# Image 1's front stepped inside image 0's depthwise convolution, in a two-layer metaformer kernel

## The chip, the cores and the metric

The kernel runs on one core of a Trainium2 chip. The metric is device time in microseconds (us) from launch to end; the shown time of a kernel is the median of its runs. A core has five engines with a queue each, and each works through its queue in order: PE (TensorE, matrix multiplies and transposes), DVE (VectorE), ACT (ScalarE), POOL (GpSimd, which here also issues the indirect DMAs) and SP (SyncE, which issues most other DMAs).

## The reference, cut to what matters

Input is x, 4 images of 384 channels by 32 x 32 points (1024 tokens an image). Two layers follow each other:

```python
# layer 0
x = x + attention(ln_c(x))            # 8 heads, relative tables, projection w_proj + b_proj
t = to_tokens(x)
t = t + gelu(ln_t(t) @ kron(c_fc_1, c_fc_2).T) @ kron(c_proj_1, c_proj_2).T
x = from_tokens(t)
# layer 1
y = ln_c(x)
x = x + dw7x7(y) + dw5x3(y) + dw3x5(y) + dw1x7_7x1(y) + dw1x5_5x1(y) + bias
t = to_tokens(x)
p = softmax(ln_t(t) @ gate_w + gate_b)            # 4 experts, the top two kept, renormalised
t = t + sum over the two experts of p * (gelu(ln_t(t) @ w1[e]) @ w2[e])
```

All five depthwise convolutions together are one 7 x 7 depthwise convolution per channel: 49 taps.

## The kernel before, in words

The first 1500 us or so are attention. All that the change touches is in `rest_phase`, which does the rest for one image after another. Channels lie on partitions in three chunks of 128 (`KC`); an image's tile `xb` is 128 x 3 x 1024, its two halves of 512 tokens are worked one after the other.

For each image:

- **front**: `loads` brings the attention output (`at`) and the image (`xb`). `project` does nine matmuls for a half (`proj_ps`, L977) and adds the result to `xb` on DVE (L980, three times); `token_stats` transposes rows on PE (`row_ps`, L87), takes statistics on DVE (L89, L90), a square root on ACT (L96). `net` spreads the scales over partitions (`all_ps`, L117, from `s_dg`, L115), then does the small network of layer 0: `u_ps` (L999, L1001), twelve f matmuls (L1012) with a gelu each on ACT (L1022), twelve o matmuls (L1016), three ffn matmuls (L1029) and adds on DVE (L1030).
- **normalise**: statistics again and `xc` (L1061), the centred half. **image** writes `xc` times its scale into `img` (L1068), the padded image. There is one `img` for all images, so an image's write stands behind the last tap of the image before.
- **convolve**: DVE adds the bias (L1080), then runs 49 taps in place, a multiply-add per chunk and tap (L1085). For images 0 to 2 a store to `x2_d` follows (L1094).
- **gates**: gate matmuls (L661), logits (L673), statistics of the rows, softmax and the choice of two experts on DVE. **scatter**: the slot of each token (`pos`, L778), the list of blocks (`block_list`), and sixteen indirect DMAs on POOL (L1197) that write the normalised rows into their slots.
- **blocks**: a block is 128 slots of one expert. An indirect DMA fetches rows (L1241), PE transposes them (`xT_ps`, L1254), two indirect DMAs fetch weights (L1260), then twelve rounds of three matmuls into `e_ps` (L1292), a gelu on ACT (L1295) and one matmul into `y_ps` (L1270); DVE adds the bias (`yo`, L1273), SP stores it. There are 67 blocks, in groups of 13, 16, 16 and 22. A group holds the blocks that the images up to its own fill; what isn't full goes to the next. So group 1 needs image 1's scatter.

Image 0 is special (`first`). DVE does chunk 0 (32 rows of 32 points) and 4 rows (`own`) of chunk 1: 36 of 96 rows. The other 60 are done by PE (`taps_by_matmul`), in four parts: two of 16 rows of chunk 2, and two of 14 rows of chunk 1. A part is 49 taps by two halves of the partitions, 98 matmuls with 64 x 64 diagonals (`tap_ps`, L1129). At its end ACT copies the two sums (L1139), PE joins them (`taps_ps`, L1140), ACT copies that (L1144) and POOL adds it to `xb` (L1145). The sums, the joins and the blocks share the PSUM pool `ps_y` ("y" twice, "t" once).

Images 1 to 3 run as `others`, a generator that is stepped from within other work. Two things set the order. Python runs the generators and so writes the program; a scheduler then orders the instructions of each engine when the kernel is built, within their dependencies. In the part with blocks, each round calls `more`, which adds 1.36 to one clock and lets `others` run until its own steps' costs (what they yield) reach it. In `others` the convolution of image b carries, from its third tap on, the dispatch (gates and scatter) of image b - 1, and from its 13th tap on the front and normalisation of image b + 1. Image 1's front and normalisation stand at the head of `others`: two steps of it (its loads) run within image 0's convolution, the rest within image 0's dispatch, three steps per step of that.

The names: `halves` is the list of (xc, scale) that `normalise` fills and `image` uses; `preload(wts[1])` fetches block weights into the tiles that held the tap diagonals; `banks` in `net` lists the PSUM banks that the f matmuls rotate through, six for images 0 and 1 and three for images 2 and 3.

Of the kernel before, what the change touches and what calls it, by code (L numbers as in the profile page):

```python
# [1 line left out]

# [1 line left out]

# [14 lines left out]
P = 128  # L19
# [874 lines left out]
def rest_phase(tc, cst, x, ao_d, ins, xs_d, y_d, x2_d, out):  # L894
# [9 lines left out]
    with ExitStack() as es:  # L904
# [82 lines left out]

        def net(b, xs, rstd):

            banks = [(ps_h, "h", None)] * 3 + ([(ps_y, "y", 2)] * 2 + [(ps_y, "t", None)] if b <= 1 else [])  # L990
            if True:
                scale = to_partitions(nc, (small, ps_m, "m"), ident, one, rstd)
                scale_sb = work.tile([P, TOK], F32, tag="scale", name="scale")
                nc.scalar.copy(scale_sb, scale)


                ps = ps_m.tile([P, TOK], F32, tag="m", name="u_ps")
                for k in range(KC):
                    nc.tensor.matmul(ps, fold[:, k, :], xs[:, k, :], start=(k == 0), stop=(k == KC - 1))  # L999
                u = small.tile([P, TOK], F32, tag="u", name="u")  # L1000
                nc.vector.tensor_tensor(u, ps, scale_sb, ALU.mult)  # L1001
                yield 1.4, 3.5

                po = ps_m.tile([P, TOK], F32, tag="m", name="o32_ps")
                pend = []
                for f0 in range(0, NF + 3, 3):
                    phs = []
                    for f in range(f0, min(f0 + 3, NF)):
                        pool, tag, bufs = banks[f % len(banks)]
                        ph = pool.tile([P, TOK], F32, tag=tag, name="f_ps", **({"bufs": bufs} if bufs else {}))  # L1010
                        lo = f % 4 * 32
                        nc.tensor.matmul(ph, c1t[lo : lo + 32, f // 4, :], u[lo : lo + 32, :], start=True, stop=True)  # L1012
                        phs.append((f, ph))
                    for f, hs in pend:
                        lo = f % 4 * 32
                        nc.tensor.matmul(  # L1016
                            po[lo : lo + 32, :], cp1t[:, f, :], hs, start=(f < 4), stop=(f >= NF - 4)
                        )
                    pend = []
                    for f, ph in phs:  # L1020
                        hs = hid.tile([P, TOK], F32, tag="hs", name="hs", bufs=HS)
                        nc.scalar.activation(hs, ph, AF.Gelu)  # L1022
                        pend.append((f, hs))
                    yield 0.0, 2.2
                o32 = small.tile([P, TOK], F32, tag="u", name="o32")
                nc.scalar.copy(o32, po)
                for m in range(KC):
                    ps = ps_h.tile([P, TOK], F32, tag="h", name="ffn_ps")
                    nc.tensor.matmul(ps, spread[:, m * P : (m + 1) * P], o32, start=True, stop=True)  # L1029
                    nc.vector.scalar_tensor_tensor(  # L1030
                        xs[:, m, :], ps, cp2[:, m : m + 1], xs[:, m, :], ALU.mult, ALU.add
                    )
                yield 2.1, 2.7
# [31 lines left out]
        def image(halves):  # L1065
            rows = IMG // 2
            for half, (xc, scale_sb) in enumerate(halves):
# [5 lines left out]
                )  # L1073
                yield 1.7, 0.0

        def convolve(b, xb, parts):


            for k in range(KC):
                nc.vector.tensor_scalar_add(xb[:, k, :], xb[:, k, :], cbias[:, k : k + 1])  # L1080
            acc = xb.rearrange("p k (y x) -> p k y x", x=IMG)
            for dy in range(7):
                for dx in range(7):
                    for k, y0, y1 in parts:
                        nc.vector.scalar_tensor_tensor(  # L1085
                            acc[:, k, y0:y1], img[:, k, dy + y0 : dy + y1, dx : dx + IMG],
                            w7[:, k, dy, dx : dx + 1], acc[:, k, y0:y1], ALU.mult, ALU.add,
                        )

                    if b:  # L1090
                        tc.keep_in_program_order(nc.vector.memset(pause, 0.0))
                    yield sum(0.12 + 0.0337 * (y1 - y0) for _, y0, y1 in parts) + 0.06, 0.0
            if b + 1 < B:
                nc.sync.dma_start(x2_d[:, b * N : (b + 1) * N].rearrange("(k p) n -> p k n", p=P), xb)  # L1094
# [10 lines left out]
        def taps_by_matmul(xb, parts):  # L1105
# [15 lines left out]
            for k, y0, ny in parts:  # L1121
                n = ny * IMG
                sums = [ps_y.tile([P, TOK], F32, tag="y", name="tap_ps", bufs=2) for _ in range(2)]
                for t0 in range(0, 49, 2):
                    for t in range(t0, min(t0 + 2, 49)):
                        dy, dx = divmod(t, 7)
                        for h in range(2):
                            lo = 64 * h
                            nc.tensor.matmul(  # L1129
                                sums[h][64 * (t % 2) : 64 * (t % 2) + 64, :n].rearrange("p (y x) -> p y x", x=IMG),  # L1130
                                diag[k][lo : lo + 64, t, :],
                                img[lo : lo + 64, k, dy + y0 : dy + y0 + ny, dx : dx + IMG],
                                start=(t < 2), stop=(t > 46),
                            )
                    yield
                po = ps_y.tile([P, TOK], F32, tag="t", name="taps_ps")
                for h in range(2):
                    e = hid.tile([P, TOK], F32, tag="hs", name="taps", bufs=HS)
                    nc.scalar.copy(e[:, :n], sums[h][:, :n])  # L1139
                    nc.tensor.matmul(po[64 * h : 64 * h + 64, :n], half, e[:, :n], start=True, stop=True)  # L1140
                yield
                acc = xb[:, k, y0 * IMG : y0 * IMG + n]
                e = hid.tile([P, TOK], F32, tag="hs", name="taps", bufs=HS)
                nc.scalar.copy(e[:, :n], po[:, :n])  # L1144
                nc.gpsimd.tensor_tensor(acc, acc, e[:, :n], ALU.add)  # L1145
                yield

        def new(shape, name, dt=F32):
# [213 lines left out]
                    yield 0.3, 0.1  # L1362
                finish(b, n0, xr, zs)

        xbs = {}

        def enter(b):
            xbs[b] = xp_.tile([P, KC, N], F32, tag="xb", name="xb")
            yield from front(b, xbs[b])

        def dispatch(b, pause=0.0):
            yield from gates(b)
            yield from scatter(b, pause)

        def first(halves):


            half, own = IMG // 2, 4
            rest = (IMG - own) // 2
            taps = taps_by_matmul(  # L1380
                xbs[0], [(2, 0, half), (2, half, half), (1, own, rest), (1, own + rest, rest)]
            )
            next(taps)
            yield from image(halves)
            for _ in convolve(0, xbs[0], [(0, 0, IMG), (1, 0, own)]):
                for _ in range(3):
                    next(taps, None)
                yield
            for _ in taps:
                pass  # L1390
            preload(wts[1])

        def others():
# [1 line left out]

            def ahead(b, halves):
                if b < B:
                    yield from enter(b)  # L1400
                    yield from normalise(xbs[b], halves)

            halves, side = [], iter(())
            yield from ahead(1, halves)
            for b in range(1, B):
                yield from image(halves)
                reached.add(b)
                halves = []
                later = ahead(b + 1, halves)
                for t, cost in enumerate(convolve(b, xbs[b], [(k, 0, IMG) for k in range(KC)])):  # L1410
                    for start, steps in ((2, side), (12, later)):
                        more = next(steps, None) if t >= start else None
# [2 lines left out]
                    yield cost  # L1415
                yield from side
                yield from later
                side = dispatch(b, 0.0 if b + 1 < B else 2.6)
            yield 6.0, 0.0
            yield from side  # L1420

        for k in range(KC):
            nc.vector.tensor_scalar_mul(fold[:, k, :], fold[:, k, :], cf2[:, k : k + 1])
        center(nc, ps_m, "m", one, fold)
        xbs[0] = xp_.tile([P, KC, N], F32, name="xb", tag="xb")
        xs0, xs1 = halves_of(xbs[0])
        halves = []
        at0, at1 = result(loads(0, xbs[0]))
        preload(wts[0], pin)
        rstd0 = result(project(xs0, at0))  # L1430
        rstd1 = result(project(xs1, at1))
        result(net(0, xs0, rstd0))
        side = normalise(xbs[0], halves, (0,))
        for _ in net(0, xs1, rstd1):
            next(side, None)
        result(side)
        result(normalise(xbs[0], halves, (1,)))
        nc.gpsimd.memset(img, 0.0)
        for _ in combined:
            pass  # L1440
        center(nc, ps_m, "m", one, gw)
        reached = set()
        todo = others()
        for i, _ in enumerate(first(halves)):
            if 6 <= i < 8:
                next(todo)
        for i, _ in enumerate(dispatch(0)):
            for _ in range(3 if i > 5 and 1 not in reached else 0):
                next(todo)
        clock = [0.0, 0.0]  # L1450

        def spend(steps):
# [126 lines left out]
```

## Time and profile before

| what | value |
|---|---|
| median of 3 runs | 3124.05 us (3121.32 to 3129.54) |
| the profiled execution | 3131.71 us |
| its span, first to last instruction | 3129.8 us |
| granted TensorE clock, mean | 0.973 |
| PE busy | 2944.8 us, 94% |
| DVE busy | 1924.3 us, 61% |
| ACT busy | 1381.9 us, 44% |
| POOL busy | 1223.7 us, 39% |

In the profiled execution image 0's convolution begins at about 1588 us and its gates at 1688.2; the first round of a block starts at 1775.7, group 1's at 2110.0. In the 344 us from 2110 to 2454 PE is busy 334.6 us.

How to read what follows. A row of a timeline or of the groups has the engine, the line of the kernel, the operation, then output <- inputs by the program's names, then partitions x elements of output and input, then how many instructions are pooled in the row. In a timeline the first two numbers are the start and the time to the end of the last of the pooled instructions, in us from the start of the span; the bracket is the idle time before and the instruction that ended it. A row of windows has a stretch and its length, and for PE, weight loads (PEld), DVE, ACT and POOL the busy time with the number of instructions; then the granted clock of PE as a share of full speed, the share of time the DMA engines were busy, and GB/s. A PE instruction in float32 appears as two records.

### The profile page before, as it was taken

The numbers are of one execution on the slowest core, as the hardware profiler recorded it, in microseconds if no ns is written. First come the engines' busy times: TensorE is split into PE (matmuls) and PEld (weight loads), VectorE is DVE, ScalarE is ACT, GpSimd is POOL, SyncE is SP. The second block draws the span as 40 slices with busy tenths as digits, with TensorE's granted clock in tenths as the row PEclk, the third lists the DMA queues.
The fourth block names the chain that finished last, engine by engine and source line by source line (L and its number), as shares of the span: only waits on it lengthen the run. The fifth ranks groups of instructions, "written<-read, shape, count | busy, mean of one in ns | idle before, by whom it ended". The sixth has DMA issues, their size and how long they took to land.

```text
span 3129.8 us, 63805 instructions
## 1 busy us (share of the span) xinstructions
PE 2944.8 (94%) x25591; PEld 2040.5 (65%) x25591; DVE 1924.3 (61%) x3572; ACT 1381.9 (44%) x2845; POOL 1223.7 (39%) x1136
## 2 busy tenths in 40 slices
PE   8997999999999999999898889989999899999996
PEld 4544777777777776777443354764777677777775
DVE  2226787878787878787485499999999500001101
ACT  1105767666666666666312313333343332333332
POOL 2224747474746464646243221230253322114412
PEclk9998999999999999999999889999999899999998
DMA  3796566666565646563412131630454145366742
GB/s 125 260 319 201 134 202 136 204 133 202 133 204 131 210 125 204 131 206 101 160 54 94 64 114 74 257 112 8 172 187 162 49 165 207 143 251 225 289 175 73
DMA packets 262792, 500.56 MB, mean 160 GB/s; under 512 B 134736, under 2 KB 186832, under 8 KB 254816
## 3 DMA queue, kind: packets, MB, share of 16 engines
q1 hardware_dynamic: 169168, 247.12, 25.5%
q0 software_dynamic: 43424, 227.84, 19.7%
q10 hardware_dynamic: 49904, 21.53, 3.5%
q8 instruction: 201, 3.29, 0.4%
q14 instruction: 95, 0.78, 0.1%
HBM read 543.58 MB, written 152.37 MB: 222 GB/s over the span
## 4 chain that ended last, share of the span: by engine, by line
PE 73%; DVE 9%; issue 8%; POOL 4%; DMA 3%; ACT 2%; another core or an unknown queue 1%; SPq 0%; POOLq 0%; DVEq 0%; ACTq 0%
PE e_ps L1292 15%; PE y_ps L1270 14%; PE t_ps L410 8%; PE sc_ps L227 7%; PE av_ps L227 7%; PE tabq_ps L227 6%; DVE xb L1085 5%; PE a_ps L420 4%; PE qk_ps L175 3%; PE tv_ps L227 2%; POOL xb L1145 2%; PE tabk_ps L227 1%; PE v_ps L186 1%; PE row_ps L87 1%; DVE oT L479 1%
## 5 line engine op out<-in xcount | busy, mean ns | idle before, releaser
L1292 PEld LDWEIGHTS e_ps<-xT,w 128*128 128x128 f32 x4824 | 658.5, 194 | 232.5 <-issue 20.4
L353 POOL TENSOR_TENSOR bias<-b,s 128x416 f32<-128x416 f32 (+24 forms) x656 | 659.4, 1044 | 172.9 <-DMA s<-sd 152.7
L1292 PE MATMUL e_ps<-xT,w 128*128 128x128 f32 x4824 | 677.0, 278 | 21.3 <-DVE xb L980 8.0
L1270 PE MATMUL y_ps<-w,eh 128*128 128x384 f32 x1608 | 655.0, 492 | 18.6 <-ACT eh L1295 16.7
L1295 ACT ACTIVATE eh<-e_ps,w 128x128 f32<-128x128 f32 x804 | 292.9, 367 | 762.8 <-PE e_ps L1292 696.4
L1085 DVE SCALAR_TENSOR_TENSOR xb<-img,pack,xb 128x1024 f32<-128x1024 f32 (+1 forms) x539 | 610.2, 1190 | 0.0
L1260 POOL DMA_INDIRECT w<-in_w,row x134 | 164.3, 1226 | 795.6 <-PE y_ps L1270 270.9
L402 DVE TENSOR_REDUCE extra<-arow 128x32 f32<-128x32 f32 (+24 forms) x768 | 380.9, 553 | 9.8 <-ACT arow L391 5.8
L381 DVE CUSTOM_DVE_ANT_0 arow<-sc_ps,bias 128x1024 f32<-128x1024 f32 x256 | 312.5, 1221 | 100.2 <-issue 50.6
L410 PEld LDWEIGHTS t_ps<-ident,arow 128*128 128x128 f32 x2048 | 220.4, 142 | 174.6 <-ACT aT L411 100.6
L391 ACT ACTIVATE arow<-arow,nm 128x1024 f32<-128x1024 f32 x256 | 302.6, 1182 | 68.0 <-DVE nm L381 68.0
L411 ACT COPY aT<-t_ps 128x512 f32<-128x512 f32 x512 | 278.5, 603 | 93.7 <-PE t_ps L410 93.4
L1273 DVE TENSOR_TENSOR yo<-y_ps,w 128x384 f32<-128x384 f32 x67 | 37.0, 553 | 451.6 <-PE y_ps L1270 441.9
L410 PE MATMUL t_ps<-ident,arow 128*128 128x128 f32 x2048 | 282.5, 281 | 16.3 <-ACT arow L391 16.3
L227 PE MATMUL sc_ps<-kk,qs 48*32 48x512 f32 x4096 | 278.7, 607 | 6.0 <-DVE nm L381 5.3
L1270 PEld LDWEIGHTS y_ps<-w,eh 128*128 128x128 f32 x1608 | 249.6, 194 | 32.1 <-ACT eh L1295 19.4
L227 PEld LDWEIGHTS av_ps<-aT,vb 128*64 128x64 f32 x4096 | 222.3, 137 | 51.3 <-ACT aT L411 40.4
L227 PE MATMUL av_ps<-aT,vb 128*64 128x128 f32 x4096 | 237.7, 274 | 0.0
L318 DVE STREAM_TRANSPOSE b<-tabk_ps 128x480 f32<-128x480 f32 x256 | 218.4, 982 | 23.4 <-PE tabk_ps L227 22.2
L227 PE MATMUL tabk_ps<-tab,kq 48*128 48x480 f32 x512 | 223.0, 582 | 6.2 <-DVE b L318 6.2
L227 PE MATMUL tabq_ps<-tab,kq 48*128 48x480 f32 x512 | 220.1, 579 | 2.1 <-ACT aT L411 1.4
L322 ACT COPY st<-tabq_ps 128x480 f32<-128x480 f32 x256 | 142.4, 560 | 71.2 <-PE tabk_ps L227 45.0
(212 smaller groups left out, 3257.9 us busy)
## 6 DMA issues: line engine op xcount, KB each, us to landing
sd<-st SPq DMA_DIRECT2D x128, 480.0 KB
s<-sd SPq DMA_DIRECT2D x256, 240.0 KB
xs_d<-zero POOLq DMA_DIRECT2D x8, 3072.0 KB
tvw<-in_tv SPq DMA_DIRECT2D x120, 192.0 KB
y_d<-yo SPq DMA_DIRECT2D x67, 192.0 KB
qk_d<-qk_sb POOLq DMA_DIRECT2D x48, 256.0 KB
qs<-qk_d SPq DMA_DIRECT2D x256, 48.0 KB
kq<-qk_d ACTq DMA_DIRECT2D x56, 192.0 KB
```

The source lines that it names most:

```text
L227: ins = nc.tensor.matmul(*args, **kw)
L318: turn = nc.vector.transpose(b2.rearrange("p e y x -> p x (e y)")[:, i + j], ps[:, j, : SPAN * IMG])
L353: nc.gpsimd.tensor_tensor(bias[:, y0:y1, :], bass.AP(b2.tensor, b2.offset + (e * IMG + y0) * IMG, [list(b2.ap[0]), [(step * IMG + 1) * IMG ...
L381: nc.vector.tensor_tensor_reduce(s["flat"], ps.rearrange("p h n -> p (h n)"), s["bias"].rearrange("p y x -> p (y x)"), -SCALE, BIG, ALU.ad ...
L391: nc.scalar.activation(s["flat"], s["flat"], AF.Exp, bias=s["nm"], scale=-1.0, accum_out=dn[:, y % YT : y % YT + 1])
L402: pin(nc.vector.tensor_reduce(ex[:, i, :], a[:, p0:p1, :].rearrange("p y x -> p x y"), AX.X, ALU.add))
L410: pin(nc.tensor.transpose(pt[:, j, :], s["flat"][:, k0 : k0 + P], ident))
L411: pin(nc.scalar.copy(aT[:, 4 * g : 4 * g + 4, s["y"] % YB, :], pt))
L1085: nc.vector.scalar_tensor_tensor(acc[:, k, y0:y1], img[:, k, dy + y0 : dy + y1, dx : dx + IMG], w7[:, k, dy, dx : dx + 1], acc[:, k, y0:y1 ...
L1270: nc.tensor.matmul(py, hs, w[:, o : o + C], start=(ff == 0), stop=(ff == NF - 1))
L1292: nc.tensor.matmul(ph, w[:, o : o + P], xT[k][:, c, :], start=(c == 0), stop=(c == KC - 1))
L1295: nc.scalar.activation(hs, ph, AF.Gelu, bias=w[:, o : o + 1])
```

## The change

Five edits, in the functions named above.

1. Image 1's front and normalisation leave `others` and become a generator, `ahead(1)`, that `first` steps within image 0's convolution: one step after each tap for five taps of seven, and all that is left (of the tap parts too) after the last tap. The taps by matmul are now stepped two at a time, every fourth time three, instead of three.
2. DVE does 8 rows of chunk 1 for image 0 (`own = 8`), 40 of 96. The last two tap parts have 12 rows (n = 384) instead of 14 (n = 448).
3. A tap part's join is added to `xb` by DVE from PSUM (the new L1147); ACT's copy (L1144) and POOL's add (L1145) go.
4. Image 1's write into `img` is called at the first step of image 0's dispatch; image 2's front and normalisation, `ahead(2)`, are stepped three at a time in the rest of that dispatch, and drained behind it. The convolution of image 1 carries neither a dispatch nor a front then; that of image 2 carries dispatch 1 and front 3; that of image 3 carries dispatch 2.
5. Image 1's three bias adds, which precede its taps, are queued with `tc.issue_after` behind a mark: the last DVE instruction that the dispatch of image 0 had written at its eleventh step, the one with the block list. The six PSUM banks in `net` are given to images 0 and 2 instead of 0 and 1.

```diff
-            banks = [...] * 3 + ([...] if b <= 1 else [])
+            banks = [...] * 3 + ([...] if b in (0, 2) else [])
...
+        def latest(engine):
+            return next(i for i in reversed(nc.cur_bb.bb.instructions) if i.engine == engine)
...
-            for k in range(KC):
-                nc.vector.tensor_scalar_add(xb[:, k, :], xb[:, k, :], cbias[:, k : k + 1])
+            with tc.issue_after(marks[b]) if b in marks else nullcontext():
+                for k in range(KC):
+                    nc.vector.tensor_scalar_add(xb[:, k, :], xb[:, k, :], cbias[:, k : k + 1])
...
-                e = hid.tile([P, TOK], F32, tag="hs", name="taps", bufs=HS)
-                nc.scalar.copy(e[:, :n], po[:, :n])
-                nc.gpsimd.tensor_tensor(acc, acc, e[:, :n], ALU.add)
+                nc.vector.tensor_tensor(acc, acc, po[:, :n], ALU.add)
...
+        def ahead(b, halves):
+            if b < B:
+                yield from enter(b)
+                yield from normalise(xbs[b], halves)
...
-            half, own = IMG // 2, 4
+            half, own = IMG // 2, 8
...
-            for _ in convolve(0, xbs[0], [(0, 0, IMG), (1, 0, own)]):
-                for _ in range(3):
+            for i, _ in enumerate(convolve(0, xbs[0], [(0, 0, IMG), (1, 0, own)])):
+                for _ in range(2 + (i % 4 == 3)):
                     next(taps, None)
+                if i % 7 < 5:
+                    next(later, None)
+                if i == 48:
+                    for steps in (taps, later):
+                        for _ in steps:
+                            pass
                 yield
-            for _ in taps:
-                pass
             preload(wts[1])
...
             for b in range(1, B):
-                yield from image(halves)
-                later = ahead(b + 1, halves)
+                if b > 1:
+                    yield from image(halves[b])
+                side, later = later, ahead(b + 1, halves[b + 1]) if b > 1 else iter(())
...
-                side = dispatch(b, 0.0 if b + 1 < B else 2.6)
+                later = dispatch(b, 0.0 if b + 1 < B else 2.6)
...
-        for i, _ in enumerate(first(halves)):
-            if 6 <= i < 8:
-                next(todo)
+        for _ in first(halves[0], ahead(1, halves[1])):
+            pass
+        after_it = ahead(2, halves[2])
         for i, _ in enumerate(dispatch(0)):
-            for _ in range(3 if i > 5 and 1 not in reached else 0):
-                next(todo)
+            if i == 0:
+                result(image(halves[1]))
+            if i == 10:
+                marks[1] = latest(mybir.EngineType.DVE)
+            for _ in range(3 if i > 5 else 0):
+                next(after_it, None)
+        result(after_it)
```

In the order that the scheduler builds from this, `others` loses image 1's write and image 2's front; image 1's gates come on PE in the last two blocks of group 0. From the second block of group 1 on, the order of PE's instructions is the same in both kernels.

More of the change, by code (lines that the diff above doesn't have):

```diff
@@ L1 @@
-from contextlib import ExitStack
+from contextlib import ExitStack, nullcontext
 import numpy as np
@@ L988, in net @@
         def net(b, xs, rstd):
-            banks = [(ps_h, "h", None)] * 3 + ([(ps_y, "y", 2)] * 2 + [(ps_y, "t", None)] if b <= 1 else [])
+            banks = [(ps_h, "h", None)] * 3 + ([(ps_y, "y", 2)] * 2 + [(ps_y, "t", None)] if b in (0, 2) else [])
             if True:
@@ L1363, in combine @@
                 finish(b, n0, xr, zs)
-        xbs = {}
+        xbs, marks = {}, {}
         def enter(b):
@@ L1373, in dispatch, with first @@
             yield from scatter(b, pause)
-        def first(halves):
-            half, own = IMG // 2, 4
+        def ahead(b, halves):
+            if b < B:
+                yield from enter(b)
+                yield from normalise(xbs[b], halves)
+        def first(halves, later):
+            half, own = IMG // 2, 8
             rest = (IMG - own) // 2
@@ L1384, in first @@
             yield from image(halves)
-            for _ in convolve(0, xbs[0], [(0, 0, IMG), (1, 0, own)]):
-                for _ in range(3):
+            for i, _ in enumerate(convolve(0, xbs[0], [(0, 0, IMG), (1, 0, own)])):
+                for _ in range(2 + (i % 4 == 3)):
                     next(taps, None)
+                if i % 7 < 5:
[4 more added lines that the diff above has]
+                            pass
                 yield
-            for _ in taps:
-                pass
             preload(wts[1])
         def others():
[L1398 to L1404, printed above, removed]
+            later = iter(())
             for b in range(1, B):
-                yield from image(halves)
-                reached.add(b)
-                halves = []
-                later = ahead(b + 1, halves)
+                if b > 1:
+                    yield from image(halves[b])
+                side, later = later, ahead(b + 1, halves[b + 1]) if b > 1 else iter(())
                 for t, cost in enumerate(convolve(b, xbs[b], [(k, 0, IMG) for k in range(KC)])):
@@ L1417, in others @@
                 yield from later
-                side = dispatch(b, 0.0 if b + 1 < B else 2.6)
+                later = dispatch(b, 0.0 if b + 1 < B else 2.6)
             yield 6.0, 0.0
-            yield from side
+            yield from later
         for k in range(KC):
@@ L1426, in rest_phase @@
         xs0, xs1 = halves_of(xbs[0])
-        halves = []
+        halves = [[] for _ in range(B + 1)]
         at0, at1 = result(loads(0, xbs[0]))
@@ L1432, in rest_phase @@
         result(net(0, xs0, rstd0))
-        side = normalise(xbs[0], halves, (0,))
+        side = normalise(xbs[0], halves[0], (0,))
         for _ in net(0, xs1, rstd1):
@@ L1436, in rest_phase @@
         result(side)
-        result(normalise(xbs[0], halves, (1,)))
+        result(normalise(xbs[0], halves[0], (1,)))
         nc.gpsimd.memset(img, 0.0)
@@ L1441, in rest_phase @@
         center(nc, ps_m, "m", one, gw)
-        reached = set()
         todo = others()
-        for i, _ in enumerate(first(halves)):
-            if 6 <= i < 8:
-                next(todo)
+        for _ in first(halves[0], ahead(1, halves[1])):
+            pass
+        after_it = ahead(2, halves[2])
         for i, _ in enumerate(dispatch(0)):
-            for _ in range(3 if i > 5 and 1 not in reached else 0):
-                next(todo)
+            if i == 0:
[5 more added lines that the diff above has]
+        result(after_it)
         clock = [0.0, 0.0]
```

## The prediction

> **What bounds the kernel now.** I read the share of each engine first (PE 94%, DVE 61%), then the chain of waits, then the stretches of the timeline that the edit touches. The chain says that TensorE sets the end almost everywhere:
>
> ```profile
> PE 73%; DVE 9%; issue 8%; POOL 4%; DMA 3%; ACT 2%; another core or an unknown queue 1%; SPq 0%; POOLq 0%; DVEq 0%; ACTq 0%
> ```
>
> DVE and POOL come into it in two places: the convolution of image 0, and the way from image 1's convolution to the first block of group 1. In image 0's convolution the timelines of DVE, POOL, ACT and PE (start, duration, line; in brackets the idle time before and what ended it) show one hand-over:
>
> ```profile
> 1589.97 71.55 DVE L1085 SCALAR_TENSOR_TENSOR xb<-img,pack,xb 128x128 f32<-128x128 f32 x98
> ...
> 1609.41 54.45 POOL L1145 TENSOR_TENSOR xb<-xb,taps 128x512 f32<-128x512 f32 x2 [80.38 <-ACT taps L1144]
> ...
> 1665.65 1.13 POOL L1145 TENSOR_TENSOR xb<-xb,taps 128x448 f32<-128x448 f32 x1 [1.80 <-ACT taps L1144]
> ...
> 1662.67 0.53 ACT L1139 COPY taps<-tap_ps 128x448 f32<-128x448 f32 x1 [9.88 <-POOL xb L1145]
> ...
> 1663.25 1.75 PE L1140 MATMUL taps_ps<-taps,half 128*64 128x448 f32 x2 [9.45 <-ACT taps L1139]
> 1664.94 21.27 PE L1129 MATMUL tap_ps<-img,w 64*64 64x448 f32 x196
> 1688.21 3.80 PE L661 MATMUL gate_ps<-xb,pack 128*32 128x512 f32 x12
> ```
>
> DVE is busy with taps to 1661.5. The second POOL add lasts until DVE is done, ACT's copy waits for that add, and PE waits 9.45 us for the copy. Gates of image 0 start at T0 = 1688.2. The way to group 1 (image 2's write, image 1's slots, the first fetch, the first block):
>
> ```profile
> 2000.42 3.42 DVE L1068 TENSOR_TENSOR img<-xc,scale 128x1536 f32<-128x1536 f32 x2
> ...
> 2075.66 0.16 DVE L778 CAST pos<-p_fpos 128x16 uint32<-128x16 f32 x1
> ...
> 2104.30 0.87 PE L1254 MATMUL xT_ps<-ident,xg 128*128 128x128 f32 x3 [7.67 <-DMA xg<-xs_d,slot]
> ...
> 2109.99 1.50 PE L1292 MATMUL e_ps<-xT,w 128*128 128x128 f32 x12
> ```
>
> PE waits there for a fetch that hangs on DVE's queue. From 2110 to 2454 PE is busy 334.6 of 344 us, and from the second block of group 1 on (block 15 of 67) both kernels issue PE's work in the same order. So **the end moves by as much as group 1's start moves**, less what PE has already done of the work behind it.
>
> **The change, part by part.**
>
> *Image 0's convolution, DVE.* 40 rows of 96 instead of 36. A pair of taps (1024 and 128 elements) takes 71.55 / 49 = 1.46 us, the 1024 one 1.20, so the 128 one 0.26. The 256 one lies between 0.26 and twice that; at 0.39 (the slope of 1024 against 128, 0.13 per 128) 49 pairs take 78.1 us: +6.6. Four L1145 adds come over, 0.66 to 0.75 us each by the L980 rows (also 512 elements with a PSUM operand): +2.8.
>
> *Taps on PE.* Two parts keep n=512; two go from 448 to 384. A full part took 21.8 and 19.7 us at 512 and 448, so 17.6 at 384 (same step): 2 x 2.1 saved. The POOL add goes, and with it the 9.45 us hold.
>
> Why POOL took 53 us for one add bears on what its removal is worth. [...] The add here outlasts all DVE's taps, so I go by the row.
>
> *Image 1's front and normalisation, moved in beside the taps.* On PE this is, by the rows of the same steps elsewhere in the trace: projection 2 x 8.0, transposes of rows 4 x 2.0, broadcasts 6 x 0.9, nets 2 x 13.7 (u 2.7, twelve f 4.2, twelve o 4.2, ffn 2.7): 56.8 us. Before, they stood between T0 and 1776, inside image 0's gates and slots, with PE busy 72.1 of 88 us (the first busy time of the row):
>
> ```profile
> 1688.00:1776.00 88.00, 72.10 (x271) 28.80 (x271) 35.55 (x155) 33.95 (x59) 25.88 (x26) 0.90 0.34 118
> ```
>
> So PE's time until image 0's gates is now 75.6 (taps: 18.6 for the 84 matmuls of the first part left at 1587.8, 21.8, 2 x 17.6) + 9.1 (joins at the four parts' ends, about 2.3 each) + 56.8 = 141.5 us. That alone, from 1587.8, puts the gates at 1729.3, while DVE, with 78 of pairs and some 15 of front work, is through its pairs by about 1685. PE is the longer of the two here.
>
> *Waits that come with it.* In the built order of DVE the third L980 of half 0 stands behind 23 pairs of taps, and the row transposes of that half wait for it on PE, with tap matmuls behind them. PE is there at 1613.9, DVE at 1590 + 23 x 1.593 + 1.6 (two L980 and a little) = 1628.2: **14.4 us**. PE's time there is 1587.8 + 82 tap matmuls x 0.2215 + 8.0 of projection. For half 1 the same walk gives 1652.9 against 1659.7, 6.8 us. Statistics, square roots and the bits of normalisation that PE waits for: about 6, from the gaps in 1688 to 1776 (between 0 and that stretch's 16). After its 9.45 us hold PE was granted a lower clock (columns: length, busy time of PE, weight loads, DVE, ACT, POOL, then the granted clock, 0.76 and 0.55, DMA share and GB/s), and the part behind it took 21.3 instead of 19.7:
>
> ```profile
> 1650.00:1660.00 10.00, 3.14 (x22) 0.92 (x14) 10.00 (x15) 0.53 (x1) 10.00 (x1) 0.76 0.00 0
> 1660.00:1670.00 10.00, 6.75 (x38) 2.18 (x42) 1.51 (x3) 1.06 (x2) 4.99 (x3) 0.55 0.00 0
> ```
>
> So 1.6 us for each of two long holds, 3.2. [...] Sum: T1 = 1729.3 + 27.2 + 3.2 = **1759.7**, 71.5 later than T0. Bounds: no holds 1729; the same with half again as much hold 1775.
>
> *From T1 to group 1.* Before, the slots' last cast came 28.7 us behind the first gate matmul, with six L980 between. Now three L980 of image 2 stand there, and their loads land in time (they follow the store of image 0 and the end of its last projection, by T1 + 20): again 28.5. The three biases behind the block list are a wait within DVE's own queue; behind them stands conv 1, which the block list precedes in any case. With them (2.1) and two more L980 the first tap of image 1 is at T1 + 32.7. Then 49 x 3.60 = 176.4 for the taps, about 20 for what is left of image 2's front and normalisation on DVE, 4.3 for eight block outputs, 2 for small things, 5 for waits on PE: image 2 is written at T1 + 240.4. (Before: T0 + 312.2, as image 1's front came between.) From there to image 1's positions it took 75.2, with 48 taps between; the new order has 63 (+18.0), three L980 (+2.2) and more statistics (+2.6): 98. Positions to first transpose as before, sixteen scatter writes and a fetch: 2104.3 - 2075.7 = 28.6. So the first transpose of group 1 is at 1759.7 + 240.4 + 98 + 28.6 = 2126.7, against 2104.3: **+22.4**. Of the PE work that stood behind it, three projection matmuls (2.7) and three transposes of rows (0.7) are now ahead, and PE waits about 1 for ACT's copy instead: **+20.0**.
>
> Meanwhile image 0's blocks start some 75 us later (before: 1775.7) and end by about 2065 (13 x 15.8); apart from a projection and rows, PE then stands idle 40 to 50 us. The front that used to fill such time has gone ahead of the gates.
>
> The profiled execution took 3131.7 us (span 3129.8); +20 gives 3152. It lies 7.7 above the median of runs, 3124.05; from the median, **3144**.
>
> **Rivals.** *(a) The front really hides: faster.* If PE passes the two row transposes without a hold (the third L980 reached first, shorter pairs), T1 is 1729, and with conv 1 free of its 5 us of waits too, the shift is 20 - 30.7 - 5 = -15.7: 3108 (3113 with those waits). It decides at T1 = 1740, that is where the long holds in image 0's taps sum to under 11 us. For it: by sums, DVE has 45 us less to do in the stage than PE. Against: the order in DVE's queue, in which nothing overtakes.
>
> *(b) An ACT hold strikes in the new place.* The trace has stops of ACT whose releaser it doesn't know, in image 1's front while image 0's scatter ran (total, times, longest):
>
> ```profile
> ACT hs L1022 <- remote: 13.8, 3, 6.5
> ```
>
> They are in the 312 us of before and not in my 240. If they come again in image 2's net, +13.5: 3157; with holds half as long again in the taps, 3166.
>
> *(c) Half of the holds,* because tap matmuls in front of the waiting transposes run slower or the pairs faster than I have them: T1 1740 to 1749, a shift of 0 to +9, say 3129, no change by the measure.
>
> *(d) The change doesn't hide the join:* the L1147 add of the first part stands behind all 49 pairs, and the second part's join needs its bank. By my times both get there near 1687; 9.45 as before if PE is early by that, and it is part of T1's bounds.
>
> **How the numbers follow.** Forecast with (d) 0.45, (b) 0.17, (c) 0.22, (a) 0.16. About 0.3% (9.4 us) is what a measurement can tell from no change: faster is below 3114.7, slower above 3133.4. (a) gives faster 0.16, (c) same 0.22, the others slower 0.62. The range from 3110 to 3164 takes in these cases, leaving half of (a) and the far end of (b) outside.
>
> **What would show it.** The first gate matmul at 1760 (not 1730); two waits of PE row transposes on L980 of 14 and 7 us; no POOL add of 50 us; image 2 written near 2000; positions of image 1 near 2098; PE idle some 40 us before group 1's first transpose at 2127; from there the same PE rows, shifted. I am wrong if PE isn't held in the taps, or if PE is not idle ahead of group 1.

## The result, and the profile after

The changed kernel takes 3141.17 us (median of 6 runs, 3137.74 to 3143.09), the kernel before 3126.36 beside it (6 runs, 3120.91 to 3131.48): ratio 1.0047, interval 1.0033 to 1.0061, **14.8 us slower**. The profiled execution has a span of 3139.3 us at a mean clock of 0.971.

The chain of waits of the changed kernel, by engine. Against the kernel before, DVE's share goes from 9 to 7% and "issue" (time in which the profile shows no wait) from 8 to 9%; PE's stays at 73%, POOL's at 4%.

```profile
PE 73%; issue 9%; DVE 7%; POOL 4%; DMA 4%; ACT 2%; another core or an unknown queue 0%; SPq 0%; POOLq 0%; ACTq 0%; DVEq 0%
```

What the change did is seen in PE's timeline within image 0's convolution (start, time to the end of the pooled instructions, line, operation, in brackets the idle time before and who ended it):

```profile
1619.08 0.33 PE L87 MATMUL row_ps<-ident,xb 128*128 128x128 f32 x1 [0.99 <-DVE xb L980]
1625.71 0.47 PE L87 MATMUL row_ps<-ident,xb 128*128 128x128 f32 x1 [6.30 <-DVE xb L980]
1631.14 1.75 PE L87 MATMUL row_ps<-ident,xb 128*128 128x128 f32 x7 [4.96 <-DVE xb L980]
1632.83 1.97 PE L1133 MATMUL tap_ps<-img,w 64*64 64x512 f32 x2
...
1664.69 1.76 PE L87 MATMUL row_ps<-ident,xb 128*128 128x128 f32 x7 [5.20 <-DVE xb L980]
1666.37 1.97 PE L1133 MATMUL tap_ps<-img,w 64*64 64x512 f32 x2
...
1764.50 2.77 PE L661 MATMUL gate_ps<-xb,pack 128*32 128x512 f32 x12
```

PE waits at the transposes of rows for the three L980 of image 1's first half one after the other, 12.25 us in all, and 5.2 us for the second half's. In DVE's timeline they stand among the taps:

```profile
1618.27 0.75 DVE L980 SCALAR_TENSOR_TENSOR xb<-proj_ps,pack,xb 128x512 f32<-128x512 f32 x1
1624.90 0.75 DVE L980 SCALAR_TENSOR_TENSOR xb<-proj_ps,pack,xb 128x512 f32<-128x512 f32 x1
1630.33 0.75 DVE L980 SCALAR_TENSOR_TENSOR xb<-proj_ps,pack,xb 128x512 f32<-128x512 f32 x1
```

Two stretches of the same trace, the first hold and all of image 1's convolution up to its slots' positions (length, busy time of PE, weight loads, DVE, ACT, POOL, then PE's clock, DMA share, GB/s):

```profile
1619.00:1640.00 21.00, 9.66 (x20) 3.32 (x20) 19.00 (x30) 1.37 (x3) 0.00 (x0) 0.54 0.00 0
...
1850.00:1900.00 50.00, 49.16 (x293) 38.15 (x292) 49.90 (x61) 17.89 (x43) 8.89 (x6) 1.00 0.10 33
1900.00:2000.00 100.00, 100.00 (x616) 79.81 (x616) 100.00 (x116) 30.21 (x81) 22.57 (x18) 1.00 0.64 243
2000.00:2097.00 97.00, 81.82 (x455) 58.88 (x454) 95.96 (x179) 31.83 (x72) 9.85 (x6) 0.92 0.37 142
2097.00:2130.00 33.00, 3.81 (x9) 1.39 (x7) 27.60 (x59) 0.75 (x2) 25.21 (x21) 0.60 0.28 102
```

DVE is full from 1850 to 2097 (busy 245.9 of 247 us), PE has almost nothing to do from 2097 to 2130 (busy 3.8 of 33). The way to group 1:

```profile
1999.87 3.41 DVE L1068 TENSOR_TENSOR img<-xc,scale 128x1536 f32<-128x1536 f32 x2
...
2096.96 0.17 DVE L778 CAST pos<-p_fpos 128x16 uint32<-128x16 f32 x1
...
2128.61 0.90 PE L1256 MATMUL xT_ps<-ident,xg 128*128 128x128 f32 x3 [28.71 <-DMA xg<-xs_d,slot]
2130.08 1.65 PE L1294 MATMUL e_ps<-xT,w 128*128 128x128 f32 x6 [0.57 <-ACT xT L1257]
```

All experiments are read by the same four marks, in us from the first tap of image 0 (in this trace 1592.81, in that of before 1589.97, so that attention's small differences stay out): gates of image 0, image 2 written, positions of image 1, first transpose of group 1. The marks are of one execution each, the medians of all runs. The runs came in sets at different times, and each ratio is to the runs of before in the same set.

| kernel, set | gates 0 | image 2 | positions 1 | group 1 | median us | ratio to before in that set (95%) |
|---|---|---|---|---|---|---|
| before, result and set 1 | 98.2 | 410.5 | 485.7 | 514.3 | 3126.4, 3124.2 | 1 |
| changed, result | 171.7 | 407.1 | 504.2 | 535.8 | 3141.2 | 1.0047 (1.0033 to 1.0061) |
| add_only, set 1 | 96.9 | 402.6 | 477.9 | 506.6 | 3119.7 | 0.9987 (0.9975 to 1.0000) |
| own8_add, set 1 | 100.5 | 407.9 | 483.1 | 511.7 | 3124.1 | 1.0000 (0.9990 to 1.0011) |
| join_h, set 1 | 79.7 | 388.1 | 463.3 | 492.1 | 3104.1 | 0.9927 (0.9914 to 0.9941) |
| proj_first, set 1 | 181.0 | 414.9 | 510.6 | 542.0 | 3147.3 | 1.0074 (1.0061 to 1.0087) |
| before_b, sets 3 and 2 | 96.9 | 390.3 | 465.5 | 494.1 | 3090.5, 3088.5 | 1 |
| after_b (changed), set 3 | 173.1 | 404.3 | 501.4 | 532.9 | 3125.3 | 1.0118 (1.0102 to 1.0133) |
| order_kept, set 2 | 151.2 | 390.2 | 485.9 | 517.4 | 3108.2 | 1.0065 (1.0053 to 1.0077) |
| order_kept_b, set 3 | 152.4 | 391.2 | 487.0 | 518.4 | 3110.9 | 1.0071 (1.0057 to 1.0085) |
| front2_back, set 2 | 172.5 | 422.2 | 511.9 | 544.4 | 3134.1 | 1.0147 (1.0132 to 1.0162) |
| no_mark, set 2 | 173.0 | 397.0 | 506.0 | 537.0 | 3126.6 | 1.0118 (1.0102 to 1.0134) |
| front_only, set 2 | 178.6 | 410.9 | 508.0 | 539.4 | 3128.7 | 1.0133 (1.0119 to 1.0148) |
| join_h_b, set 3 | 79.7 | 370.9 | 446.1 | 474.8 | 3070.5 | 0.9939 (0.9925 to 0.9952) |

In sets 2 and 3 before takes 3088.5 and 3090.5 us instead of 3124. Some of the expectations below put this down to a second chip. The record doesn't bear that out: it numbers the chip 14 in set 1, 10 in set 2 and 14 again in set 3. So I speak of sets, called earlier (the result and set 1) and later (2 and 3), and what differs between them isn't known.

### The profile page after: what moved, and what is told of

Its sections match the earlier page's. It is cut to its first block, busy times and chain, and to the rows that moved or that the text cites. A ratio compares the mean times of both kernels' runs of the same rounds, so it can differ in the third digit from the quotient of the medians.

```text
span 3139.3 us, 63791 instructions
## 1 busy us (share of the span) xinstructions
PE 2942.2 (94%) x25591; PEld 2026.2 (65%) x25591; DVE 1935.2 (62%) x3576; ACT 1370.1 (44%) x2833; POOL 1168.1 (37%) x1132
## 4 chain that ended last, share of the span: by engine, by line
PE 73%; issue 9%; DVE 7%; POOL 4%; DMA 4%; ACT 2%; another core or an unknown queue 0%; SPq 0%; POOLq 0%; ACTq 0%; DVEq 0%
PE e_ps L1294 16%; PE y_ps L1272 15%; PE t_ps L410 7%; PE sc_ps L227 7%; PE av_ps L227 6%; PE tabq_ps L227 5%; DVE xb L1089 3%; PE a_ps L420 3%; PE tap_ps L1133 2%; DMA s<-sd 2%; PE tv_ps L227 2%; POOL bias L353 1%; PE proj_ps L977 1%; PE row_ps L87 1%; PE tabk_ps L227 1%
## 5 line engine op out<-in xcount | busy, mean ns | idle before, releaser
L1294 PEld LDWEIGHTS e_ps<-xT,w 128*128 128x128 f32 x4824 | 654.5, 192 | 214.1 <-issue 10.7
L1294 PE MATMUL e_ps<-xT,w 128*128 128x128 f32 x4824 | 669.4, 276 | 8.6 <-DVE pause L1095 2.4
L1089 DVE SCALAR_TENSOR_TENSOR xb<-img,pack,xb 128x1024 f32<-128x1024 f32 (+1 forms) x539 | 616.8, 1203 | 0.0
L1275 DVE TENSOR_TENSOR yo<-y_ps,w 128x384 f32<-128x384 f32 x67 | 37.1, 553 | 460.3 <-PE y_ps L1272 460.3
L1272 PEld LDWEIGHTS y_ps<-w,eh 128*128 128x128 f32 x1608 | 246.7, 192 | 23.6 <-ACT eh L1297 13.8
L1199 POOL DMA_INDIRECT xs_d<-rows,pos x64 | 78.5, 1227 | 337.7 <-DVE xb L980 253.0
```

Source lines behind the costliest of these rows:

```text
L1089: nc.vector.scalar_tensor_tensor(acc[:, k, y0:y1], img[:, k, dy + y0 : dy + y1, dx : dx + IMG], w7[:, k, dy, dx : dx + 1], acc[:, k, y0:y1 ...
L1272: nc.tensor.matmul(py, hs, w[:, o : o + C], start=(ff == 0), stop=(ff == NF - 1))
L1294: nc.tensor.matmul(ph, w[:, o : o + P], xT[k][:, c, :], start=(c == 0), stop=(c == KC - 1))
```

## The experiments

### Where PE is held in image 0's convolution, without any front moved

Two edits of the change alone, on the kernel before.

```diff
# add_only
-                e = hid.tile([P, TOK], F32, tag="hs", name="taps", bufs=HS)
-                nc.scalar.copy(e[:, :n], po[:, :n])
-                nc.gpsimd.tensor_tensor(acc, acc, e[:, :n], ALU.add)
+                nc.vector.tensor_tensor(acc, acc, po[:, :n], ALU.add)
# own8_add: this, and
-            half, own = IMG // 2, 4
+            half, own = IMG // 2, 8
# join_h: both, and
-                po = ps_y.tile([P, TOK], F32, tag="t", name="taps_ps")
+                po = ps_h.tile([P, TOK], F32, tag="h", name="taps_ps")
```

> The kernel before, with one edit alone: the joined tap parts are added to the image by DVE from PSUM, POOL's add and ACT's copy go. Theory (the hold is not POOL's but that of the one PSUM bank of the joins): the second part's add stands behind all 49 pairs in DVE's queue, the third part's join needs its bank, so PE is held about 11 us there instead of 9.45 behind the POOL add; gates of image 0 within 1.5 us of before, time 3126 (3122 to 3131). Rival (the POOL add was the hold, and it goes): gates 9 to 11 us earlier, time 3114 to 3117.

> The kernel before, with two edits: DVE's adds from PSUM, and 40 rows of 96 on DVE (last two parts 12 rows). Theory of the bank: pairs end 6.6 us later, so the third join is held about 20 us; gates 4 us later than before, time 3130 (3126 to 3135). Rival (a balance of work: two tap parts shorter by 2.1 each, no POOL add): gates 13 us earlier, time 3113.

> As the one before it (DVE's adds, 40 rows on DVE), but the joins take their bank from the pool with three banks. Theory of the bank: no join waits for an add of DVE, PE works 85 us through the four parts, gates 14 us earlier than before; all PE work up to the end moves with them, time 3112 (3108 to 3117). Rival (the DVE queue or something behind the gates sets the end): less than 5 us gained, 3121 or more.

PE's waits in own8_add, and DVE's timeline beside it:

```profile
1639.65 8.69 PE L1129 MATMUL tap_ps<-img,w 64*64 64x384 f32 x100
1668.26 1.55 PE L1140 MATMUL taps_ps<-taps,half 128*64 128x384 f32 x4 [19.93 <-DVE xb L1143]
```

```profile
1626.06 41.46 DVE L1085 SCALAR_TENSOR_TENSOR xb<-img,pack,xb 128x1024 f32<-128x1024 f32 x52
1667.45 0.67 DVE L1143 TENSOR_TENSOR xb<-xb,taps_ps 128x512 f32<-128x512 f32 x1
```

The second part's add stands behind the last tap, the third part's join needs the bank that this add frees, and PE waits 19.93 us, as the theory had it (20). In add_only the same wait is 10.7 (expected 11). Gates moved by -1.3 and +2.3 us, the times by -4.5 and 0. Both rivals wanted the gates 9 to 13 us earlier, and are out by that. The time alone would not settle it for add_only: its 3119.7 lies between the theory's 3122 and the rival's 3117. The times came out 6 below what I expected of the theory for both. The marks show where: from gates to image 2 these traces took 305.7 and 307.4 us, that of before 312.2. The stops of ACT told of further below are part of it (the last six gelus of image 1's first half took 19.5 and 18.8 us in them, 21.7 in before); the rest is open.

With three banks no join waits for DVE, gates come 18.5 us earlier than in before and the end 20.1. PE's timeline in join_h shows what is left:

```profile
1609.47 22.01 PE L1129 MATMUL tap_ps<-img,w 64*64 64x512 f32 x196
1632.21 1.56 PE L1140 MATMUL taps_ps<-taps,half 128*64 128x512 f32 x4 [0.73 <-ACT taps L1139]
1633.70 16.59 PE L1129 MATMUL tap_ps<-img,w 64*64 64x384 f32 x196
...
1670.46 2.77 PE L661 MATMUL gate_ps<-xb,pack 128*32 128x512 f32 x12
```

The gates gain 4.5 us more than the 14 I expected. Some 3 of it is that a 12-row part takes 16.59 us instead of my 17.6 and a join of 384 costs 1.8 with its gap instead of 2.3 (one of 512 costs 2.2). The end moves with the gates, and a little more. In set 3 join_h_b gains 20.0 (gates 17.2, group 1 19.3 earlier):

> The kernel before with DVE's adds, 40 rows on DVE and the joins in the pool of three banks; no front moved. Theory (a wait of PE for a bank in image 0's convolution goes, and all PE work behind it moves with it): gates 80 us after the first tap, time 14 to 20 under before on either chip. Rival (its gain on the first chip came from ACT's stops falling elsewhere): on a chip without them under 8.

This is the version that beats both kernels, by 0.6 to 0.7% against before, and no front is moved in it.

### Taking the holds out of the changed kernel

First try: proj_first steps both halves' projections before any statistics, and the statistics later.

```diff
-            for xs, at in zip(halves_of(xb), ats):
-                rstds.append((yield from project(xs, at)))
+            parts = [project(xs, at) for xs, at in zip(halves_of(xb), ats)]
+            if b == 1:
+                for part in parts:
+                    for _ in range(KC):
+                        yield next(part)
+            for part in parts:
+                rstds.append((yield from part))
...
-                if i % 7 < 5:
+                if i in (*range(11), 22, *range(32, 49)):
                     next(later, None)
```

> The changed kernel, with image 1's six projection groups and their adds ahead of its statistics, and the statistics of the halves stepped 12 and 16 taps later, so that the transposes of rows reach PE when DVE has the adds done; nothing is left out. Theory (the two long holds at the transposes of rows make the gates of image 0 late, and the end follows): both holds (12 and 5 us) go, one of about 9 appears at a later broadcast; gates 10 to 13 us earlier than in the changed kernel, time 3129 (3125 to 3133). Rival (the end of the changed kernel hangs on the convolution of image 1 and not on image 0's gates): 3138 to 3142.

Neither came: it is 23 us over the runs of before beside it, where the changed kernel was 15 over its own. The L980 were in time, but the next DVE instruction in line was not:

```profile
1645.97 1.07 PE L1138 MATMUL tap_ps<-img,w 64*64 64x512 f32 x2
1668.75 0.90 PE L87 MATMUL row_ps<-ident,xb 128*128 128x128 f32 x3 [21.70 <-DVE s_st L89]
1669.58 1.97 PE L1138 MATMUL tap_ps<-img,w 64*64 64x512 f32 x2
```

Three transposes fill the pool's three banks, the fourth waits until DVE has taken the first's statistics, and those stand behind all 49 pairs: 21.7 us. I had left that bank out of my walk. The kernel does not tell the theories apart in the way meant, but gates 9.3 us later than in the changed kernel, group 1 6.2 later and the end some 6 to 8 later fit the theory: a wait of PE in this stage reaches the end.

Second try: order_kept puts every pair behind the DVE instructions that the program had written before it.

```diff
-                    for k, y0, y1 in parts:
-                        nc.vector.scalar_tensor_tensor(
+                    with nullcontext() if b else tc.issue_after(latest(mybir.EngineType.DVE)):
+                        for k, y0, y1 in parts:
+                            nc.vector.scalar_tensor_tensor(
...
```

> The changed kernel, with each pair of image 0's taps queued on DVE behind the last DVE instruction that the program had written, so that image 1's projection adds and statistics are no longer overtaken by taps; PE's order up to image 0's gates is the same as in the changed kernel. Theory (DVE's queue order holds PE in image 0's convolution; gates and end follow it one to one): the first adds come 7 to 8 taps earlier, the holds at the transposes of rows go, gates some 150 us after the first tap instead of 171.7; end 18 to 24 us earlier than the changed kernel, 3119 (3114 to 3125). Rival (PE is simply full there, or something behind the gates sets the end): 3135 to 3142.

> The changed kernel with DVE's program order kept in image 0's convolution, beside the changed kernel on one chip. Theory (DVE's queue holds PE there): gates 151 us after the first tap against 172, time 18 to 24 below the changed kernel. Rival (PE is full there): within 5 of the changed kernel.

PE's timeline of order_kept_b at the two places where the changed kernel was held:

```profile
1613.58 1.20 PE L87 MATMUL row_ps<-ident,xb 128*128 128x128 f32 x9
1614.71 1.07 PE L1134 MATMUL tap_ps<-img,w 64*64 64x512 f32 x2
...
1637.46 1.20 PE L87 MATMUL row_ps<-ident,xb 128*128 128x128 f32 x9
1638.59 1.10 PE L1134 MATMUL tap_ps<-img,w 64*64 64x512 f32 x2
```

No bracket: both holds are gone, in the same order of PE's work up to the gates (but for eight records of broadcasts and taps late in the stage). Gates come 20.7 us earlier than in after_b (152.4 against 173.1; expected 151 against 172), the time is 14.4 lower beside it (3110.9 against 3125.3). So PE was not full there. (order_kept, in set 2, has no run of the changed kernel beside it; its ratio of 1.0065 agrees with order_kept_b's.) Of the 20.7 us, 14.5 are left at group 1: image 2 is written 238.8 us behind the gates instead of 231.2, as PE now waits 5.8 us for image 2's attention output to land (a row of its waits). I expected 18 to 24 us of the time; taking the gates' gain one to one was too much.

### What the other parts are worth

```diff
# front2_back: image 2's front again in image 1's convolution
-                side, later = later, ahead(b + 1, halves[b + 1]) if b > 1 else iter(())
+                side, later = later, ahead(b + 1, halves[b + 1])
...
-        after_it = ahead(2, halves[2])
...
-            for _ in range(3 if i > 5 else 0):
-                next(after_it, None)
-        result(after_it)
# no_mark
-                marks[1] = latest(mybir.EngineType.DVE)
+                pass
# front_only: own = 4, and ACT's copy and POOL's add as before
```

> The changed kernel, with image 2's front and normalisation back in the convolution of image 1, as before; image 1's front stays in image 0's convolution. Theory (from the gates of image 0 on, DVE's queue sets group 1's start, and its work is the same either way): blocks of image 0 start some 40 us earlier, group 1 and the end stay, 3141 (3135 to 3146). Rival (the late start of the blocks is what costs): 3124 or less.

> The changed kernel without the mark: image 1's bias adds and first taps may pass image 0's gates and block list on DVE. Theory (DVE's chain sets group 1): the taps fill some 5 to 8 us of DVE's idle time between the gates and the first tap, the block list comes 10 to 15 us later without harm; 3135 (3131 to 3139). Rival (the list's lateness delays the blocks, and the end with them): 3145 or more.

> The changed kernel with 36 rows on DVE and POOL's add as before: only image 1's and image 2's fronts move. Theory: the joins come too late to wait for POOL's add, so the old hold is gone without the DVE add; the two longer tap parts cost 4.2 us, and the adds of image 1's first half stand 1 to 2 taps later in DVE's queue, some 5 us of hold: 3149 (3143 to 3156). Rival (POOL's add holds the joins as it did before): 3158 or more; rival (edits 2 and 3 give nothing beside the front): 3141.

These three ran in set 2, where before is 2 us off set 3, so they are held against after_b (3125.3, ratio 1.0118) and not against the times that I expected, which were those of set 1.

- front2_back is 9 us slower than after_b. The first block's output comes 29 us earlier (1837.4 against 1866.7) and it does not help: image 2 is written 249.7 us behind the gates instead of 231.2, since DVE now waits for PE within image 1's convolution (busy 195.8 of the 215 us from 1796 to 2011). The rival, that the late start of the blocks costs, is out; that group 1 and the end would stay where they are was wrong by 11.5 and 9 us.
- no_mark can't be told from after_b (1.0118 both). Neither the gain of 6 nor the loss came. Group 1's first transpose is 4.1 us later in its trace, of which 1.3 are left at the output of block 20: the mark changes nothing measurable in the time.
- front_only is 3.4 us over after_b, with overlapping intervals; gates 5.5 later. Expected were 8 by the theory and 0 by the second rival; the runs leave that open. The first rival is out: POOL's four adds took 1.1 to 1.3 us each. The first of them began at 1634.11 in a pause of DVE (2.10 us, DVE waiting for ACT's square root), the others behind the last pair; in before the same add began within the unbroken row of taps and lasted 53.2.

### The same change in a later set

> The kernel before once more, for a trace from the same chip as the three beside it. On a chip where ACT stops without a known releaser as in the first trace (13.8 us in image 1's front, 9.5 later): 3124, group 1's first transpose 514 us after image 0's first tap. On a chip where before runs in 3088, the theory (those ACT stops are the difference) expects stops of under 3 us, the same 98 us to the gates, and group 1's first transpose about 500 us after the first tap. Rival (that chip is faster everywhere, PE's work above all): stops as before, each stretch shorter by about 1%.

> The changed kernel once more. On a chip with the ACT stops: 3141, 15 over before. On one without them the theory (the change escapes before's 13.8 us stop in image 1's front, since that front no longer runs beside image 0's scatter, and this had hidden part of its cost) expects 28 to 40 over before, 3116 to 3129. Rival (the ACT stops play no part in the difference): 15 over before there too, 3103.

Before's traced run took 3085.9, the changed kernel 3125.3 (4 runs): **34.8 us slower** than the nine runs of before beside it, inside the 28 to 40 that the theory gave and far from the rival's 15. The changed kernel reaches its marks almost alike in both sets (gates 171.7 and 173.1, group 1 535.8 and 532.9). Before does not: from gates to image 2 it took 312.2 us in the earlier trace and 293.4 in the later. The last f matmul of image 1's first half and ACT's gelus behind it, in the earlier trace:

```profile
1727.22 1.13 PE L1012 MATMUL f_ps<-u,pack 32*128 32x512 f32 x6
...
1729.88 0.60 ACT L1022 ACTIVATE hs<-f_ps 128x512 f32<-128x512 f32 x1 [4.28 <-PE f_ps L1012]
1732.00 0.60 ACT L1022 ACTIVATE hs<-f_ps 128x512 f32<-128x512 f32 x1 [1.52 <-remote]
1738.33 0.60 ACT L1022 ACTIVATE hs<-f_ps 128x512 f32<-128x512 f32 x1 [5.74 <-remote]
1745.46 1.81 ACT L1022 ACTIVATE hs<-f_ps 128x512 f32<-128x512 f32 x3 [6.54 <-remote]
```

The twelve gelus in the later trace:

```profile
1717.48 3.04 ACT L1022 ACTIVATE hs<-f_ps 128x512 f32<-128x512 f32 x6 [1.45 <-PE f_ps L1012]
1721.31 1.57 ACT L1022 ACTIVATE hs<-f_ps 128x512 f32<-128x512 f32 x3 [0.78 <-PE f_ps L1012]
1723.36 1.57 ACT L1022 ACTIVATE hs<-f_ps 128x512 f32<-128x512 f32 x3 [0.48 <-PE f_ps L1012]
```

Stops whose releaser the profile doesn't know ("remote") make 13.8 us there, against none. With them PE waits (its o matmuls 12.1 us for ACT), and its clock in the stretch from 1688 to 1776 is 0.90 against 1.00. The last six of the gelus, with all their gaps, take 21.7 us in the earlier trace and 4.4 in the later. Matched instruction by instruction, the two traces are 5.1 us apart at the gates and 24.0 at image 1's first L1030, right behind these gelus: that is all of the 18.8 between 312.2 and 293.4. In join_h the same six take 19.5 us with only 6.5 called "remote", and 4.4 in join_h_b, so the name alone understates the loss.

No such stop is in the later traces of before_b, after_b, order_kept_b, join_h_b, front2_back, no_mark and front_only. Of the earlier, the four kernels with image 1's front in its old place have 12 to 23 us of them in all, the changed kernel and proj_first 5.7 and 5.3, from about 2500 us on, among the blocks. So in the earlier runs the change also escaped a stall that struck image 1's front only in its old place, and this hid more than half of its cost. What releases ACT is not in the trace, and no run here settles it, nor why those later traces are free of it. Nor is all of the sets' difference told by it: behind group 1's first transpose before was 21.8 us faster in the later trace and the changed kernel 12.8. Of those 9 the named stops there, 9.5 and 5.7 us, make 3.8, and I have not traced the rest.

## Why the prediction was right

It said 3144 us at 0.62 for slower; measured 3141. By its own steps:

- **The end follows group 1's start.** By the blocks' outputs (L1275, counted from 0) the shift between the two traces is constant from block 21 to 27 at 17.3 to 17.4 us; 2.8 of it is the later first tap, which leaves 14.5, beside 14.8 for the medians. In the profiled executions it shrinks later to 9.6, as the one of before lies 5.4 us above its median, so that the two figures agree this well is partly luck. The traces of set 3 show the rule more plainly: between before_b and after_b the shift is 36.5 us at block 21 and 37.8 from block 31 to the last.
- **Gates of image 0.** Said: 1759.7, 71.5 later than before; measured 73.5 later (171.7 - 98.2). The sum was right, two terms were not, and that they offset each other is luck. Tap matmuls took 89.3 us, not 75.6. In join_h_b, where they run in one piece, the same 378 took 73.8, in order_kept_b, broken up by the front's matmuls but not held, 86.1: so 12.3 for the breaking up, and the other 3.2 come with the holds and the low clock there (0.54 from 1619 to 1640, 0.57 from 1660 to 1672). Holds and clock, on the other hand, were 30.4 in the sum; the trace has 19.65 us of idle PE in the stage, of which 17.4 are the two holds (12.25 and 5.2; said: 14.4 + 6.8).
- **Gates to image 2** 235.4, said 240.4. **To positions** 97.1, said 98. **To the first transpose** 31.6, said 28.6, with PE idle for 28.7 us ahead of it, said some 40. Group 1 starts 21.5 later from the first tap, said 22.4.
- **PE's work already done at that point**: said 2.4 net, measured 8.1 by the output of the group's first block (16.2 later against 24.3 at the transpose; by block 21 it is 7.0). This is the term that makes the forecast 3 to 5 us too high.
- **The POOL add goes, and with it the 9.45 us hold**: wrong as said. The add that lasts until DVE is done is the first of the four (53.2 us), not the second (1.26). add_only shows that the hold turns into one of 10.7 behind DVE's own queue, and join_h that it is the bank of the joins. It is absent in the changed kernel, and with it rival (d), only because the front's matmuls make the joins late (three of the four wait 0.6 to 0.7, for ACT), so the sum came out.
- **Rival (a)**, the front really hides: its condition, holds below 11 us, was not met (17.4). order_kept met it, with gates at 151 to 152 instead of the 139 that (a) had, since the taps were dearer, and is still 20 us slower than before in the later sets: image 1's front within the taps is not hidden work but PE work ahead of the gates (PE is busy 145.4 of the 152.4 us in order_kept_b). The break-even at T1 = 1740 leaned on the stops in before's trace: 14 us under the changed kernel would have been about before's time in the earlier set (an estimate, as order_kept didn't run there), and it is 20 us over it in the later ones. **Rival (b)**, ACT stops in the new place: none came in image 2's net.

Taken as a difference the range reaches from -14 to +40 us, so it also holds the +34.8 of set 3; the forecast of +20 doesn't come near it. The stops of ACT are why: some 19 us of before's 312 were theirs, and I gave them no price of their own. That 3144 came within 3 us of the result is in this part luck, as it needed runs in which before had the stops in image 1's front.

## What to carry to other kernels

Ask for each moved instruction behind what it stands on its own engine's queue, and also for the buffer that it must free: here three of the fixes (add_only, own8_add, proj_first) turned one PE wait into another of 10 to 22 us behind the same DVE taps, and giving the joins a pool of three banks (join_h against own8_add) took off 20 us, where the whole change added 15. Filling an engine's idle time pays only if what it fills stands off the path: image 1's front went in front of image 0's gates, while the idle time came back later, ahead of group 1. A gain or loss below 1% should be measured again in a later set of runs, where a stall may be missing that one of the two kernels happened to meet: here the same change cost 14.8 us in one and 34.8 in another.

## What the runs showed of the hardware

- A tap matmul (64 columns of weights, 512 of data, two records) costs 0.22 us in a long run of its kind (98 in 22.01 us in join_h), but 1.07 alone between transposes (order_kept_b, at a granted clock of 0.99 over the stage), and eight between projections cost 2.0 instead of 1.8. Interleaving them with the front's matmuls made the taps 17% dearer (86.1 us in order_kept_b against 73.8 in join_h_b) at a clock of 0.99 to 1.00 and with 7 us of idle PE in the whole stage.
- After the holds of 6.30 and 4.96 us the same single tap took 1.97 us instead of 1.07, which is 1.84 times as long, at a granted clock of 0.54 in that stretch (the changed kernel, 1619 to 1640).
- POOL's add of 128x512 lasted 53.2 us when it began beside an unbroken row of DVE's taps (before, from 1609.41 to 1662.6; the last tap ended at 1661.5), 1.26 when it began behind the last tap (before, the second add), and 1.27 when it began in a pause of DVE (front_only). What holds it so long, no run shows.
- ACT stopped for up to 6.5 us at a time in before's earlier trace, and not in before_b's, the same program. Its inputs were ready: in the earlier trace the last f matmul was over at 1728.35, and the last four gelus began between 1738.33 and 1746.69.
